# A graph attention and slice attention layer: the first attention's product in seven parts, its residual added by a transfer, and passes moved to ScalarE

## The chip, the core and the metric

The kernel runs on one core of a Trainium2 chip. The core has TensorE (matrix products, written to the eight banks of PSUM), VectorE (DVE in the profile), ScalarE (ACT), GpSimd (POOL), SyncE (SP), which here issues nearly all transfers, and 16 DMA engines that carry them. Each engine works through its own queue of instructions in order; semaphores hold an instruction back until what it needs is there. The metric is the device time of one execution in microseconds (us), as the median of a few runs. A profile is one further execution, recorded by the hardware.

## What is computed

The input x is 32 batches of 512 rows with 256 features, in 32-bit floats. Each batch goes through a graph part (two attentions over 512 nodes, the second masked with a 512 x 512 adjacency) and a slice attention with 8 heads of 64 slices. Both parts have a layer norm before them and x added behind.

```python
def _gat(inp, adj_mask, W, a):
    h = jnp.matmul(inp, W)
    F_ = h.shape[-1]
    f1 = jnp.matmul(h, a[:F_, 0])
    f2 = jnp.matmul(h, a[F_:, 0])
    e = jax.nn.leaky_relu(f1[:, :, None] + f2[:, None, :], ALPHA)
    if adj_mask is not None:
        e = jnp.where(adj_mask[None, :, :] > 0, e, NEG_INF)
    att = jax.nn.softmax(e, axis=2)
    h_prime = jnp.einsum('bij,bjf->bif', att, h)
    return jax.nn.elu(h_prime)
...
out = jax.nn.relu(jnp.matmul(x, mlp1_w) + mlp1_b)            # 256 -> 512
residual = out
out = _gat(jax.nn.relu(out), None, W_fc, a_fc)               # 512 x 512 nodes, 512 features
out = jax.nn.elu(out) + residual
out = jax.nn.relu(jnp.matmul(out, mlp2_w) + mlp2_b)          # 512 -> 256
residual = out
out = _gat(jax.nn.relu(out), adj, W_hand, a_hand)
out = jax.nn.elu(out) + residual
return jax.nn.relu(out)
...
slice_weights = jax.nn.softmax((x_mid @ W_slice + b_slice) / temp, axis=-1)
```

## The kernel before

**Recording and order.** The program first records every operation of all 32 batches (class `Recorder`, from line 52). Its `_cost` gives each operation an estimated duration and its `order` gives each a due time: a step of a batch is due at `TURNS[step]` after the batch's turn, with corrections for the first and last three batches (`HEAD`, `TAIL`). `_schedule` then fills each engine's queue, taking the operation with the smallest due time of those that can start; up to four batches are under way at once. `emit` issues the result. That is why nearly every instruction of the profile has line 290, where the recorded call is made, and why instructions are told apart by their tiles. The order is fixed when the program is built; on the chip each engine keeps it.

**Steps of a batch.** `front` has "load", "norm1", "mlp1", "h", "factors", "p", "pv" and "o1"; `middle` has "mlp2", "h2", "e", "p2" and "pv2"; `back` has "norm2", "w", "sums", "s1T", "tokens", "att", "vo", "gg" and "out". A matrix of 512 x 512 lies in SBUF as four blocks of 128 rows. A matmul takes a 128 x 128 block of weights and up to 512 moving columns; in 32-bit floats the profile shows two records for it.

**The first attention.** "mlp1" (line 686) makes o0T, features by nodes, which is also the residual; o0T has two buffers. "h" multiplies it with W_fc by one level of Strassen's scheme: a 2 x 2 split of both matrices, four mixed left blocks in `mix`, three mixed right blocks made once, and seven products in place of eight, whose results are copied (ScalarE) or added (VectorE, `total`) into the four parts of h. h carries one column more per half, 257 in place of 256: the products with `a` (f1, f2), and later ones, whose product is the softmax's sum. "factors" and "p" make the unnormalised softmax, transposed, as pT. "pv" is the product of pT and h: four blocks of rows, two halves of columns, four matmuls each, 32 in all, into eight PSUM tiles. Behind each block of rows, `elu_elu` scales by the reciprocal sum (one half on VectorE, one on ScalarE), takes the minimum with zero (VectorE), two exponentials (ScalarE) and the maximum (VectorE).

**Transposing by transfer.** In batches 1 to 30 `by_dma` holds: `flip` transposes blocks of 32 x 32 on VectorE into `u_stage`, and `gather` sends that in four pieces to a scratch tensor in DRAM and fetches it back in one transfer, by which blocks find their places. All five are issued by SP. In step "o1" VectorE then adds o0T to the fetched o1T, four sums of 512 columns. In batches 0 and 31 TensorE transposes and VectorE adds from PSUM. The same way goes for xn, e, o2, w and xn2.

**The second layer.** "mlp2" is a Strassen product too: four mixes of o1T, 14 matmuls of 256 columns, copies and totals into o2T, then four Relu with bias.

**The softmax of the slices.** In "w" VectorE takes the maximum of each head from PSUM, subtracts it (512 columns from PSUM to w), ScalarE takes the exponential of 512 columns, and VectorE sums, inverts and multiplies.

**Buffers the change touches.** Tiles with the same tag share buffers and follow each other. mix and pT share one buffer, e has four, o0T two, o1T one.

Of the kernel before, what the change touches and what calls it, by code (L numbers as in the profile page):

```python
# [10 lines left out]
AF = mybir.ActivationFunctionType  # L11
# [6 lines left out]
    "load": 1919.6, "norm1": 757.9, "mlp1": 2922.4, "h": 2999, "factors": 2963.5, "p": 3012.6,  # L18
    "pv": 3019, "o1": 3053.1, "mlp2": 3049.1, "h2": 3076.9, "e": 3079.2, "p2": 2878.8,
    "pv2": 3103.9, "norm2": 3107.9, "w": 3170.3, "sums": 3226, "s1T": 3182.8, "tokens": 3948.3,  # L20
    "att": 792.6, "vo": 1634.2, "gg": 326.4, "out": 996.7,
}
PERIOD, SPARE = 90.53, 0.01

HEAD = (
    (0, 381, 5, 16, 257, -146, -491, -92, -529, -621, 0, 137, -13, -48, 1, 767, 207, -242, -12,
     -51, -10, 0),
    (48, -35, -193, -5, -10, -46, 13, -151, 0, 3, 22, 0, -244, -13, -5, -639, 0, -3, -392, 11,
     -308, -28),
    (-12, 15, 17, -10, 254, 207, -865, 717, -1593, -13, -52, 114, 999, -101, -3, 681, 388, 0,  # L30
     -5, 0, -8, 0),
)
TAIL = (
    (-89, -112, -430, -582, 0, 0, -4, -68, 3, 0, -3, 0, -177, -19, 464, -878, 0, -636, -1, -19,
     33, 129),
    (-70, -57, -31, 0, 0, 0, -514, 1, 23, 200, 0, 0, -677, -169, 954, 2258, 106, -118, 57, -5,
     558, -59),
    (-4, 0, 55, 279, 38, 67, -544, -56, -8, 104, -113, 0, -104, 1, 0, 1, -53, -242, -3, 20, 48,
     166),
# [7 lines left out]
P = 128  # L47
# [4 lines left out]
class Recorder:  # L52
# [5 lines left out]
    ISSUE, BEGIN, LAND, BEHIND = 0.45, 2.2, 0.0, 3.6  # L58
# [69 lines left out]
    def _cost(self, op, out, ins):  # L128
# [6 lines left out]
        if op.method == "dma_start":  # L135
            side = next(ap for ap in (out, *ins) if ap.space != bass.MemoryType.DRAM)
            kb = out.size() / 256
            if side.ap[0][1] <= P // 4:
                op.moving = 0.3 + max(0.0, 1.08 * (kb / 128 - 1))
            else:  # L140
                op.moving = max(1.5 * kb / 512, 4.0 * kb / 1024 - 0.5)
            return self.ISSUE, 0.0
# [7 lines left out]
        if op.engine == "scalar":  # L150
            pointers = sum(isinstance(op.kwargs.get(k), bass.AP) for k in ("bias", "scale"))
            return 0.06 + n / 1200 + 0.09 * pointers + 0.19 * ("accum_out" in op.kwargs), 0.12
# [175 lines left out]
def adj_ffn_kernel(  # L328
# [71 lines left out]
    def gather(what, stage, dst):  # L400
# [5 lines left out]
        for a in range(P // Q):  # L406
# [3 lines left out]
        nc.sync.dma_start(  # L410
            dst, scr.rearrange("(k c) r a j -> (c r) k (a j)", c=P // Q)
        )
# [82 lines left out]
    mixed2 = new("mixed2", [P, 3, 2, P])  # L495
# [691 lines left out]
```

## Time and profile before

| what | value |
|---|---|
| median of 3 runs | 2523.22 us (2522.84 to 2527.05) |
| the profiled execution | 2525.8 us |
| its span, first to last instruction | 2524.0 us |
| mean granted TensorE clock | 0.994 |
| instructions | 35133 |
| DMA | 348.75 MB, 138 GB/s on average, queue 1 busy 49.2% |

The profile names an instruction by engine, operation and tiles, "output<-inputs"; groups add all instructions with the same names. A line of the timeline has the start, the duration, the engine, the line of the program, the operation and how many instructions are merged. In the rows of a group stand the time busy in all, the mean of one in ns, and the idle time before them with what ended it. In the table by stage each row gives the stage's length and, for each engine, its busy time and its instructions, then the granted TensorE clock, the DMA share and GB/s. PEld is the loading of weights, which overlaps PE. SPq is SP's queue, which issues transfers.

### The profile page before, as it was taken

The numbers are of one execution on the slowest core, as the hardware profiler recorded it, in microseconds if no ns is written. First come the engines' busy times: TensorE is split into PE (matmuls) and PEld (weight loads), VectorE is DVE, ScalarE is ACT, GpSimd is POOL, SyncE is SP. The second block draws the span as 40 slices with busy tenths as digits, with TensorE's granted clock in tenths as the row PEclk, the third lists the DMA queues.
The fourth block names the chain that finished last, engine by engine and source line by source line (L and its number), as shares of the span: only waits on it lengthen the run. The fifth ranks groups of instructions, "written<-read, shape, count | busy, mean of one in ns | idle before, by whom it ended". The sixth has DMA issues, their size and how long they took to land.

```text
span 2524.0 us, 35133 instructions
## 1 busy us (share of the span) xinstructions
PE 2470.2 (98%) x12037; PEld 1797.5 (71%) x12037; DVE 2193.6 (87%) x5593; ACT 1175.2 (47%) x2197; POOL 96.3 (4%) x167
## 2 busy tenths in 40 slices
PE   6999999999999999999999999999999999999998
PEld 4867677776777777777777776767777777767674
DVE  7779898998989988889998989988899888989784
ACT  2544444444445444445444444444454454454452
POOL 0000000000000000000000000000000000000000
PEclk8999999999999999999999999999999999999998
DMA  5133555454655445565454654546554455554431
GB/s 173 40 92 101 146 169 158 136 142 113 170 161 165 121 129 143 159 171 142 127 152 130 169 159 136 141 113 171 161 166 120 135 140 157 169 158 123 125 89 53
DMA packets 451144, 348.75 MB, mean 138 GB/s; under 512 B 110228, under 2 KB 375572, under 8 KB 450966
## 3 DMA queue, kind: packets, MB, share of 16 engines
q1 hardware_dynamic: 449382, 345.46, 49.2%
q8 instruction: 96, 1.57, 0.3%
q10 hardware_dynamic: 1584, 1.05, 0.1%
q14 instruction: 82, 0.67, 0.1%
HBM read 186.92 MB, written 159.45 MB: 137 GB/s over the span
## 4 chain that ended last, share of the span: by engine, by line
PE 77%; DMA 9%; DVE 8%; ACT 3%; SPq 1%; issue 1%; POOL 0%; DVEq 0%; ACTq 0%
PE mm L290 74%; PE tr L290 3%; DMA line<-norm 2%; DMA xn_raw<-scr 2%; DMA scr<-u_stage 1%; SPq L290 1%; DVE mix L290 1%; DVE u L290 1%; ACT m L290 1%; DVE xn_stage L290 1%; DVE xn L290 1%; DMA p2T<-scr 1%; DVE m L290 1%; DMA scr<-xn_stage 0%; DMA w<-in_L_gnn_mlp_w_dram 0%
## 5 line engine op out<-in xcount | busy, mean ns | idle before, releaser
L290 PE MATMUL mm<-h,pT 128*128 128x257 f32 (+1 forms) x2048 | 478.5, 379 | 1.3 <-DVE pT L290 1.3
L290 PEld LDWEIGHTS mm<-h,pT 128*128 128x128 f32 x2048 | 384.8, 189 | 106.5 <-issue 44.1
L290 PE MATMUL mm<-weff,xn2T 128*128 128x512 f32 x512 | 254.0, 603 | 0.5 <-ACT xn2T L290 0.5
L290 PE MATMUL mm<-w,xn 128*128 128x512 f32 x512 | 251.5, 595 | 0.5 <-DVE w L290 0.5
L290 PE MATMUL mm<-h,p2T 128*128 128x257 f32 x1024 | 242.6, 380 | 1.0 <-DMA p2T<-scr 1.0
L290 PE MATMUL mm<-xnT,w 128*128 128x512 f32 x512 | 236.3, 604 | 3.0 <-DMA xnT<-scr 2.3
L290 PE MATMUL mm<-gg,wT 128*128 128x256 f32 x1024 | 232.9, 383 | 1.6 <-DVE gg L290 1.6
L290 PEld LDWEIGHTS mm<-gg,wT 128*128 128x128 f32 x1024 | 192.3, 191 | 45.8 <-DVE gg L290 18.8
L290 PEld LDWEIGHTS mm<-h,p2T 128*128 128x128 f32 x1024 | 193.7, 190 | 42.8 <-issue 14.7
L290 ACT ACTIVATE m<-m 128x512 f32<-128x512 f32 x192 | 121.1, 631 | 188.6 <-DVE m L290 188.5
L290 PEld LDWEIGHTS mm<-xnT,w 128*128 128x128 f32 x512 | 94.7, 192 | 114.3 <-issue 99.6
L290 DVE TENSOR_TENSOR h<-mm,h 128x257 f32<-128x257 f32 x320 | 127.2, 417 | 45.9 <-PE mm L290 39.7
L290 DVE SCALAR_TENSOR_TENSOR u<-m,u 128x512 f32<-128x512 f32 x192 | 131.4, 684 | 38.9 <-ACT m L290 38.4
L290 ACT ACTIVATE u<-mm,rd 128x256 f32<-128x256 f32 x192 | 90.3, 470 | 154.8 <-PE mm L290 97.3
L290 ACT COPY h<-mm 128x257 f32<-128x257 f32 (+1 forms) x256 | 95.1, 374 | 130.4 <-PE mm L290 126.2
L290 ACT ACTIVATE w<-w 128x512 f32<-128x512 f32 x128 | 80.1, 626 | 142.4 <-DVE w L290 139.5
L290 ACT ACTIVATE m<-m,neg 128x512 f32<-128x512 f32 x192 | 138.5, 722 | 4.8
L290 ACT ACTIVATE o0T<-mm,b 128x512 f32<-128x512 f32 x128 | 87.7, 685 | 106.3 <-PE mm L290 105.6
L290 PEld LDWEIGHTS mm<-w,xn 128*128 128x128 f32 x512 | 94.9, 189 | 57.1 <-issue 44.0
L290 PE MATMUL mm<-wfc,mix 128*128 128x257 f32 x512 | 133.1, 380 | 0.0
L290 ACT COPY xn2T<-xn_raw 128x512 f32<-128x512 f32 x60 | 34.2, 616 | 202.3 <-DMA xn_raw<-scr 202.3
L290 PE MATMUL mm<-mixed,mix 128*128 128x257 f32 x512 | 125.0, 384 | 0.1
(172 smaller groups left out, 4515.7 us busy)
## 6 DMA issues: line engine op xcount, KB each, us to landing
scr<-xn_stage SPq DMA_DIRECT2D x240, 128.0 KB, 2.7
scr<-u_stage SPq DMA_DIRECT2D x120, 256.0 KB, 4.9
o1T<-scr SPq DMA_DIRECT2D x30, 1024.0 KB, 7.4
scr<-e_stage SPq DMA_DIRECT2D x120, 256.0 KB, 4.7
p2T<-scr SPq DMA_DIRECT2D x30, 1024.0 KB, 6.6
scr<-w_stage SPq DMA_DIRECT2D x120, 256.0 KB, 3.9
w_raw<-scr SPq DMA_DIRECT2D x30, 1024.0 KB, 7.9
x<-in_x_dram SPq DMA_DIRECT2D x32, 512.0 KB, 5.2
```

What stands on the lines that cost most here:

```text
L290: getattr(getattr(self.nc, op.engine), op.method)(*op.args, **op.kwargs)
```

## The change

- "pv" becomes a Strassen product as well: four mixes of pT in a new tile pmix, seven products (28 matmuls), copies on ScalarE and totals on VectorE into four tiles v, which share their buffers with e. pmix takes the buffer of o0T in batches 1 to 30, and o0T has one buffer in place of two. "h" builds the four right blocks that this needs directly (the tile hx), by another order of sums, and the column of ones becomes ones, minus ones and ones in three blocks.
- The residual: in batches 1 to 30 "mlp1" has ScalarE write its result a second time, with columns rearranged, into o1T, which now has two buffers; the gather of u goes out on GpSimd's queue with an add, and the four sums of "o1" are gone.
- "mlp2" loses its Strassen level: 8 matmuls of 512 columns, with o1T's columns read in another order, and two Relu. The mixes of its weights in the setup are gone.
- `elu_elu`: in both attentions the minimum goes from VectorE to ScalarE (a Relu of the negative, then an Exp with scale -1); the first attention's scaling is one pass on ScalarE.
- The softmax of w: no subtraction; for each head ScalarE takes an exponential of 64 columns from PSUM with the negative maximum as bias, 8 for each block of rows. One of "factors"' two products of 512 columns goes to ScalarE.
- Some small tiles share other buffers; `TURNS`, `HEAD`, `TAIL` and the estimates of `_cost` have other values, so the order of every queue differs.

```diff
-    def gather(what, stage, dst):
+    def gather(what, stage, dst, op=None):
...
-        nc.sync.dma_start(
-            dst, scr.rearrange("(k c) r a j -> (c r) k (a j)", c=P // Q)
-        )
+        whole = scr.rearrange("(k c) r a j -> (c r) k (a j)", c=P // Q)
+        if op is None:
+            nc.sync.dma_start(dst, whole)
+        else:
+            nc.gpsimd.dma_start(dst, whole, accum_op=op)
...
-    def elu_elu(parts, m, u):
-        (v0, rd0, cols0), (v1, rd1, cols1) = parts
-        nc.vector.tensor_scalar(u[:, cols0], v0, rd0, None, op0=OP.mult)
-        nc.scalar.activation(u[:, cols1], v1, AF.Copy, scale=rd1)
-        nc.vector.tensor_scalar(m, u, 0.0, None, op0=OP.min)
-        nc.scalar.activation(m, m, AF.Exp)
+    def elu_elu(m, u, to=None):
+        nc.scalar.activation(m, u, AF.Relu, scale=-1.0)
+        nc.scalar.activation(m, m, AF.Exp, scale=-1.0)
         nc.scalar.activation(m, m, AF.Exp, bias=neg1)
-        nc.vector.scalar_tensor_tensor(u, m, -1.0, u, op0=OP.add, op1=OP.max)
+        nc.vector.scalar_tensor_tensor(
+            u if to is None else m, m, -1.0, u, op0=OP.add, op1=OP.max
+        )
...
-        o0T = new("o0T", [P, KH, N], bufs=2)
+        o0T, o1T = new("o0T", [P, KH, N]), new("o1T", [P, KH, N], bufs=2)
...
             nc.scalar.activation(o0T[:, m, :], pm, AF.Relu, bias=b1[:, m : m + 1])
+            if by_dma("u", b):
+                nc.scalar.activation(
+                    swapped(o1T[:, m, :]), pm.rearrange("p (t a i) -> p t a i", t=NT, i=Q),
+                    AF.Relu, bias=b1[:, m : m + 1],
+                )
...
+        keep(h1, product(l11, r11))
+        total(h11, product(l12, r21), h1)
+        keep(h2, product(s3, t3))
+        total(h1, product(s2, t2), h1)
+        total(h1, h1, h2)
+        total(h22, product(s1, t1), h1)
+        total(h3, h2, product(s4, r22), OP.subtract)
+        total(h21, product(l22, t4), h1)
+        total(h2, h11, h3)
+        total(h1, h22, h2, OP.subtract)
+        total(h4, h21, h2, OP.subtract)
...
+        l11, l12, l21, l22 = (pT[:, ts(k, 2), ts(t, 2 * P)] for t in range(2) for k in range(2))
+        held = by_dma("u", b)
+        pmix = new(
+            "pmix", [P, 4, 2, 2 * P], tag="o0T" if held else "o1T", bufs=1 if held else 2
+        )
...
+        keep(v12, product(l11, h11))
+        total(v11, product(l12, h21), v12)
+        keep(v22, product(s1, h1[:, :, :HH]))
+        total(v12, product(s2, h2), v12)
+        for i in range(2):
+            nc.vector.tensor_copy(v21[i][:, HH:], v12[i][:, HH:])
+        total(v21, product(s3, h3[:, :, :HH]), v12)
+        total(v12, narrow(v22), v12)
+        total(v22, narrow(v21), v22)
+        total(v12, product(s4, h22[:, :, :HH]), v12)
+        total(v21, product(l22, h4[:, :, :HH]), v21)
         for i in range(NT):
-            pms = [mm_tile([P, HH + 1]), mm_tile([P, HH])]
-            for s, pm in enumerate(pms):
-                for j in range(NT):
-                    nc.tensor.matmul(
-                        pm, pT[:, j, ts(i)], h[:, j, s, : HH + 1 - s],
-                        start=(j == 0), stop=(j == NT - 1),
-                    )
             rd = small("rd", [P, 1])
...
-            gather("u", stage, o1T)
-            for m in range(KH):
-                o1 = o1T[:, m, :].rearrange("p (t a i) -> p t a i", t=NT, i=Q)
-                nc.vector.tensor_tensor(o1, o1, swapped(o0T[:, m, :]), op=OP.add)
+            gather("u", stage, o1T, OP.add)
...
+        for m in range(KD):
+            pm = mm_tile([P, N])
+            for k in range(KH):
+                nc.tensor.matmul(
+                    pm.rearrange("p (a t i) -> p a t i", t=NT, i=Q), w2[:, k, ts(m)],
+                    swapped(o1T[:, k, :]), start=(k == 0), stop=(k == KH - 1),
+                )
+            nc.scalar.activation(o2T[:, m, :], pm, AF.Relu, bias=b2[:, m : m + 1])
...
-            nc.vector.tensor_reduce(mx, pm3, axis=AX.X, op=OP.max)
-            nc.vector.tensor_tensor(
-                w3, pm3, mx[:, :, None].to_broadcast([P, HEADS, G]), op=OP.subtract
-            )
-            nc.scalar.activation(wt, wt, AF.Exp)
+            nc.vector.tensor_reduce(mx, pm3, axis=AX.X, op=OP.max, negate=True)
+            for hd in range(HEADS):
+                nc.scalar.activation(w3[:, hd], pm3[:, hd], AF.Exp, bias=mx[:, hd : hd + 1])
```

## The prediction

> **What bounds the kernel now.** I read the page's totals first, then busy time by stage, then the order of matmuls in one steady stretch, then the waits, then the transfers around the step that changes.
>
> ```profile
> PE 2470.2 (98%) x12037; PEld 1797.5 (71%) x12037; DVE 2193.6 (87%) x5593; ACT 1175.2 (47%) x2197; POOL 96.3 (4%) x167
> ...
> 0.00:300.00 300.00, 273.35 (x1219) 204.15 (x1220) 240.23 (x626) 126.97 (x238) 11.76 (x26) 0.97 0.41 113
> ...
> 1000.00:1700.00 700.00, 695.10 (x3378) 504.83 (x3377) 623.13 (x1584) 334.76 (x623) 26.69 (x45) 1.00 0.52 144
> ...
> 2200.00:2524.00 324.00, 306.98 (x1598) 218.65 (x1596) 255.79 (x641) 140.03 (x266) 8.99 (x16) 0.98 0.39 109
> ```
>
> TensorE is busy 98% of the span. In the middle stage it idles 4.9 us of 700; nearly all of its idle time is at the start (26.7 us of the first 300) and the end (17.0 of the last 324). The clock granted in the middle is 1.00. So time is the number of matmul columns, plus the two ends. A busy PE isn't yet a PE at its peak, so I price matmuls by the distance between starts:
>
> ```profile
> 1225.76 1.88 PE L290 MATMUL mm<-weff,xn2T 128*128 128x512 f32 x4
> 1227.48 0.38 PE L290 MATMUL tr<-ident,sc 128*128 128x128 f32 x2
> ...
> 1257.99 7.11 PE L290 MATMUL mm<-h,p2T 128*128 128x257 f32 x32
> 1264.94 1.88 PE L290 MATMUL mm<-w,xn 128*128 128x512 f32 x4
> ...
> 1283.41 1.89 PE L290 MATMUL mm<-o1T,w 128*128 128x256 f32 x8
> 1285.14 1.89 PE L290 MATMUL mm<-mix,mixed 128*128 128x256 f32 x8
> ```
>
> One matmul of the program is two records. 512 columns: (1227.48 - 1225.76) / 2 = 0.860 us. 257 columns: 6.95 / 16 = 0.434. 256 columns: 1.73 / 4 = 0.432. Time follows columns; only a change in columns, or a new wait, moves the end.
>
> ```profile
> PE mm L290 <- DVE o1T L290: 2.5, 4, 1.0
> ...
> 1263.36 4.75 SPq L290 DMA_DIRECT2D scr<-u_stage  x4
> ...
> 1271.42 0.37 SPq L290 DMA_DIRECT2D o1T<-scr  x1
> ...
> scr<-u_stage SPq DMA_DIRECT2D x120, 256.0 KB, 4.9
> o1T<-scr SPq DMA_DIRECT2D x30, 1024.0 KB, 7.4
> ```
>
> The transposed blocks of the first attention go out in four pieces and come back in one transfer. They are in time today: the second layer's matmuls waited 2.5 us in the whole run for o1T. But between the last product (timeline: 1257.99) and mlp2 (1283.41) lie only 25.4 us of other matmuls, and o1T's sums run at 1279.92: this is the tight place.
>
> **The change, part by part.**
>
> *TensorE.* The product of the first attention goes from 32 matmuls per batch to 28: 4 x 0.434 = 1.74 us less. mlp2 loses its own Strassen level: 14 matmuls of 256 (14 x 0.432 = 6.05 us) become 8 of 512 (8 x 0.860 = 6.88), 0.83 us more. Over 32 batches: -55.6 + 26.6 = -29.0 us. mlp2's moving operand is now read in blocks of 32 columns, which no row shows; between no effect and the 2% by which 257 columns vary here I take none (upper end +0.14 us a batch, 4 us).
>
> *VectorE.* These rows go or grow:
>
> ```profile
> L290 DVE TENSOR_SCALAR m<-u 128x512 f32<-128x512 f32 x192 | 78.9, 411 | 26.0 <-ACT u L290 25.5
> L290 DVE TENSOR_TENSOR w<-mm,mx 128x512 f32<-128x512 f32 x128 | 87.0, 680 | 0.4
> L290 DVE TENSOR_TENSOR o1T<-o1T,o0T 128x512 f32<-128x512 f32 x120 | 74.9, 684 | 1.8 <-DMA o1T<-scr 1.8
> L290 DVE TENSOR_TENSOR h<-h 128x257 f32<-128x257 f32 x128 | 51.7, 418 | 1.6
> L290 ACT ACTIVATE m<-m 128x512 f32<-128x512 f32 x192 | 121.1, 631 | 188.6 <-DVE m L290 188.5
> L290 ACT ACTIVATE ex<-ex 128x8 f32<-128x8 f32 x32 | 6.5, 202 | 22.0 <-DVE ex L290 22.0
> L290 ACT COPY mean<-mm 128x128 f32<-128x128 f32 x32 | 8.5, 265 | 19.4 <-PE mm L290 19.4
> ```
>
> Gone: o1T's sums 75, mlp2's mixes 85 (128 x 0.66) and totals 94, the minimum m<-u 79, two thirds of u<-mm,rd 60, the subtraction of w 87, acb 22: 502 us. Added: pmix 128 x 0.66 = 85, totals of v 448 x 0.40 = 179, h's totals from 448 to 576, 128 x 0.40 = 51, small ones 18: 333. Net -169: 2194 becomes some 2025, 80%. It was not the bound and moves further away. I cost this at nothing: TensorE's rows cover it. Were that cover gone, VectorE would set 2025 us, still less.
>
> *ScalarE.* Added: Relu for the minimum 192 x 0.631 = 121; the second copy of mlp1 (the residual) 120 x 0.685 = 82; acb 19; four copies of v a batch 48; the scaling of v 22 net; mlp2's two wide instead of six narrow ones -41. The softmax of w goes from 128 wide exponentials (80) to 1024 of 64 columns; no row is that narrow with a bias. Bounds: 0.20 us (the 8-column row) and 0.36 (the 128-column row plus the 0.09 by which m<-m,neg exceeds m<-m). I take 0.30: +227 (125 to 289). Sum +478: 1175 becomes 1653, 65%. Again under TensorE.
>
> A rule speaks against moving min and max: the Trainium skill, "ScalarE: Activation LUTs", Rules for kernel authors, gives relu, max and min to VectorE. By the rows it is right about price, 0.411 against 0.631; with VectorE at 87% and ScalarE at 47% the dearer engine is the freer one, so the sum by the rule (42 us lost) doesn't reach the end.
>
> *The residual's transfer.* The gather of 1 MB moves from SP's queue to GpSimd's and adds into o1T, where ScalarE has written the residual. On SP it frees one issue of 0.37. Behind it on GpSimd stand the two small operations of each layer norm (1.1 and 0.34 us), which now also wait until the four pieces have landed; the next norm's statistics come later than that in VectorE's order, so nothing. How long an adding transfer takes no row shows. Lower bound: the plain one, 7.4. Upper: two streams read instead of one, 14.8. It is one transfer of the same size between the same places, so I take it nearer the plain end, 8.
>
> The Trainium skill, "DMA: Bandwidth & Descriptors", SWDGE vs HWDGE vs iDMA, says only GpSimd's queue can accumulate; its fit for that queue (2.0 us plus bytes at 436 GB/s) would give an estimate of 4.4 us, under the plain row. "SBUF — State Buffer", SBUF: two separate sides, warns that VectorE's two-port operations hold up that queue's descriptors; by it the transfer would be later, and no row here shows it.
>
> Is it in time? After the last product the built order has 19 matmuls of 512 and 26 of 257 before mlp2: 16.3 + 11.3 = 27.6 us, some 28.4 at the middle's real pace (two batches lie 152.6 us apart in the chain of waits, 615.62 to 768.26, where these prices give 148.4). Against it: tiles 0 and 1 are ready about 0.8 us before the end of the last product (1.74 of matmuls still to come, less two totals and a reciprocal); ScalarE then runs four passes for four tiles (scale, Relu, two Exp: 0.64 + 0.63 + 0.63 + 0.72 = 2.63 each), 10.5, with some 2 us of w's narrow ones in between; VectorE's max and transposition of the last 1.4: 13.1 after the last product. Four issues of 0.46 and 4.9 to land: 6.7. The transfer, 8. Together 27.8. It just fits; I cost it at nothing, and name the price below.
>
> *The ends.* In batches 0 and 31 the transpositions of u are TensorE's and no longer interleave with the product's rows: all four tiles come after it. ScalarE's 10.5 us then stand against 7.8 us of other matmuls in batch 0 (8 x 0.86 and 8 transpositions) and about 2 in batch 31, where before only the last row's 3.6 stood open: +3 and +5 us. The setup loses five small VectorE operations (2.0 us), hidden by the loads. Together +8 (0 to +16).
>
> *Sum.* -29 + 8 = -21. The profiled execution took 2525.8 us, its span 2524.0 and 1.8 around it; it becomes 2504.8. The median of the runs is 2523.2, 2.6 under it: **2502**.
>
> **Rivals.** *The adding transfer is late* (the slower side). Place: mlp2's first matmul, in order on TensorE with everything behind it; nothing takes up a wait there, since the middle stage has 0.7% idle. Price: 30 batches x each us past 28.4, so beyond 8.6 us for the transfer the wait begins, and at 9.3 the 21 us are gone. Midway between its bounds, at 11, it is 2.4 late: 72 us, 2574. At 14.8, 6.2 late: 186, 2688. For it: the slack is under 1 us, and three 1 MB gathers share the queues there. Against: today's chain is as tight and waits 2.5 us in all.
>
> *The gain is eaten inside the product.* Seven products need 14 PSUM tiles per batch, each drained by a copy (0.37) or total (0.40) before the next sums; before, 8 with looser order. If each batch waits 0.7 us more, the time is 2523. Against: VectorE is 7 points freer, and the same scheme for h costs PE waits of only 0.2 us in the whole run.
>
> *More than the columns.* VectorE's relief also closes waits at the ends: no loss there and a quarter of their 43.7 idle us gone, 2523 - 29 - 11 = 2483.
>
> *The product isn't shorter at all*: ruled out by the built order, 28 matmuls where 32 stood.
>
> **How the numbers follow.** My forecast 0.54, more than the columns 0.10, eaten inside 0.14, late transfer 0.22. Anything within 0.2% (5 us, about what a measurement of this kernel can tell from no change) is the middle of the third case. Faster: 0.54 + 0.10 + 0.03 = 0.67; same 0.07; slower 0.22 + 0.04 = 0.26. Range: from 2480 to 2580, which takes in the late transfer up to some 2.5 us a batch; the likeliest case alone is 2490 to 2514.
>
> **What would show it.** Right: PE's records of the product 1792 instead of 2048 and mlp2's 512 of 512 columns, spacing unchanged; the middle's batches some 75.4 us apart; DVE near 80%, ACT near 65%; the page's issue list giving o1T<-scr under 8.6 us; no PE wait on o1T. Wrong: a PE wait on DMA o1T<-scr of over 1 us a batch, or PE under 97% in the middle stage.

## The result, and the profile after

The changed kernel takes 2695.35 us, median of 4 runs (2683.12 to 2701.47), against 2525.14 for the kernel before beside it (2522.84 to 2527.7): a ratio of 1.0671, with a 95% interval of 1.0637 to 1.0704. The forecast was 2502, the range 2480 to 2580. The profiled execution took 2690.28 us, its span 2688.5; with the forecast of 2504.8 for such an execution, 185.5 us are to be found.

The totals of the page, and the table by stage (length, then busy time and instructions of PE, PEld, DVE, ACT and POOL, the granted clock, the DMA share, GB/s), of the changed kernel:

```profile
PE 2496.1 (93%) x11397; PEld 1700.3 (63%) x11397; DVE 2029.3 (75%) x5532; ACT 1482.0 (55%) x3437; POOL 129.3 (5%) x197
...
0.00:300.00 300.00, 272.69 (x1177) 192.74 (x1178) 230.08 (x645) 161.81 (x343) 15.68 (x29) 0.98 0.45 115
1000.00:1700.00 700.00, 653.57 (x2929) 442.53 (x2928) 526.58 (x1436) 386.49 (x898) 35.41 (x52) 0.97 0.55 137
2364.50:2688.50 324.00, 295.67 (x1483) 199.17 (x1481) 226.19 (x593) 172.30 (x426) 10.70 (x18) 0.96 0.42 106
```

In the middle 700 us TensorE idles 46.4 us where it idled 4.9, and its clock is 0.97 where it was 1.00. By share of the whole span no engine has become the bound: TensorE and VectorE are less busy than before, and ScalarE is at 55% (by stretches of a batch it is another matter, as the experiments show). The loss is waits, and a batch takes 82.7 us (mlp1's starts, batch 4 to 28) where it took 76.5.

The waits of TensorE in the changed kernel (us in total, times, longest), then one of VectorE, then three transfers (count, KB each, median us from issue to landing):

```profile
PE mm L297 <- DMA o1T<-scr: 99.1, 26, 6.1
PE mm L297 <- DVE w L297: 27.6, 23, 2.4
PE mm L297 <- ACT xn2T L297: 11.0, 7, 6.7
...
DVE norm L297 <- DMA norm<-s1T: 168.1, 27, 8.8
...
scr<-u_stage SPq DMA_DIRECT2D x120, 256.0 KB, 4.5
o1T<-scr POOLq DMA_DIRECT2D x30, 1024.0 KB, 12.1
norm<-s1T SPq DMA_DIRECT2D x32, 2.0 KB, 10.4
```

The last of these transfers in the kernel before:

```profile
norm<-s1T SPq DMA_DIRECT2D x32, 2.0 KB, 4.5
```

(w is the softmax of the slices, xn2T the transposed result of the second layer norm.) The adding transfer takes 12.1 us where the plain one took 7.4, and mlp2 waits for it 99.1 us in all. A transfer of only 2 KB that SP issues beside it lands after 10.4 us; before it took 4.5. One batch of the changed kernel shows both. First the timeline (start, duration), then the table by stage for the stretches around the wait:

```profile
1315.89 1.89 PE L297 MATMUL mm<-hx,pT 128*128 128x256 f32 x8
...
1333.12 0.70 DVE L297 STREAM_TRANSPOSE u_stage<-m 128x512 f32<-128x512 f32 x1
1333.85 3.36 SPq L297 DMA_DIRECT2D scr<-u_stage  x4
...
1341.53 1.36 POOL L297 DMA_DIRECT2D o1T<-scr  x1 [21.92 <-ACT o1T L297]
...
1343.54 1.82 SPq L297 DMA_DIRECT2D norm<-s1T  x1
...
1353.59 3.75 PE L297 MATMUL mm<-o1T,w 128*128 128x512 f32 x4 [3.85 <-DMA o1T<-scr]
1354.00 0.17 DVE L297 TENSOR_SCALAR norm<-norm 128x4 f32<-128x4 f32 x1 [6.57 <-DMA norm<-s1T]
```

```profile
1341.50:1349.70 8.20, 8.20 (x31) 5.36 (x29) 1.80 (x4) 5.93 (x12) 1.49 (x2) 1.00 0.99 167
1349.70:1353.60 3.90, 0.05 (x2) 0.04 (x1) 0.00 (x0) 0.37 (x1) 0.00 (x0) 0.89 0.82 162
1353.60:1357.10 3.50, 3.50 (x4) 1.47 (x5) 3.10 (x9) 0.00 (x0) 0.00 (x0) 0.50 0.49 153
```

The last product ends at 1317.8, the last transposition at 1333.8 (16.0 us later, 3 more than in the median batch), the adding transfer is issued at 1341.5 and lands 11.9 later. For the last 3.9 us hardly an engine has work: TensorE stands at mlp2, VectorE at norm, in order, and both are released within half a microsecond. Then TensorE runs at half clock: this stretch lasts 6.83 us from 1352.7 on, and TensorE is at work in 5.9 us of it. This happens in nearly every batch: the trace has 31 stretches at half clock, 156.8 us in all, against 5 and 31.8 before. Of the 31, 18 are 3.41 us long and 9 are 6.83. The Trainium skill, "TensorE: Matmul & The Clock Gate", Part 1: The HAM clock gate, says that a free-running window of some 3.4 us without work halves the clock. The lengths agree with such a window. That it has to be without work does not show here, and the measurement decides: in the 3.41 us before each of the 31 drops TensorE was at work for 0 to 1.53 us, 0.74 in the median.

The difference of the spans, 2688.5 - 2524.0 = 164.5 us, is made up so: fewer columns, -29.0; TensorE's idle time (span less busy) from 53.8 to 192.4, +138.6; half clock, +51.7, since TensorE is at work in 125.5 us of the stretches at half clock, against 22.2 before, and does half as much in them: (125.5 - 22.2) / 2. In the rest of these stretches it stands anyway. The sum is 161.3, 3 short.

### The profile page after: what moved, and what is told of

Read it like the earlier page. It is cut to its first block, busy times and chain, and to the rows that moved or that the text cites. A ratio compares the mean times of both kernels' runs of the same rounds, so it can differ in the third digit from the quotient of the medians.

```text
span 2688.5 us, 35257 instructions
## 1 busy us (share of the span) xinstructions
PE 2496.1 (93%) x11397; PEld 1700.3 (63%) x11397; DVE 2029.3 (75%) x5532; ACT 1482.0 (55%) x3437; POOL 129.3 (5%) x197
## 3 DMA queue, kind: packets, MB, share of 16 engines
q0 software_dynamic: 15840, 31.46, 6.7%
## 4 chain that ended last, share of the span: by engine, by line
PE 50%; DVE 24%; DMA 18%; issue 3%; ACT 3%; SPq 1%; POOL 0%; DVEq 0%; POOLq 0%; ACTq 0%
PE mm L297 48%; DMA o1T<-scr 9%; DVE e L297 4%; DVE pT L297 2%; DMA norm<-s1T 2%; DVE v L297 2%; PE tr L297 2%; DVE e_stage L297 2%; DVE xn_stage L297 1%; DVE pmix L297 1%; DVE xn L297 1%; DMA xn_raw<-scr 1%; DMA scr<-e_stage 1%; DVE mx L297 1%; SPq L297 1%
## 5 line engine op out<-in xcount | busy, mean ns | idle before, releaser
L297 PE MATMUL mm<-o1T,w 128*128 128x512 f32 x512 | 273.9, 694 | 101.5 <-DMA o1T<-scr 99.1
L297 PE MATMUL mm<-w,xn 128*128 128x512 f32 x512 | 245.8, 604 | 28.3 <-DVE w L297 27.6
L297 ACT ACTIVATE w<-mm,mx 128x64 f32<-128x64 f32 x1024 | 249.7, 341 | 33.8 <-DVE mx L297 30.3
L297 PEld LDWEIGHTS mm<-o1T,w 128*128 128x128 f32 x512 | 111.4, 224 | 247.2 <-issue 243.1
L297 PE MATMUL mm<-h,p2T 128*128 128x257 f32 x1024 | 235.1, 383 | 2.1 <-DMA p2T<-scr 1.2
L297 ACT ACTIVATE v<-v,rd 128x512 f32<-128x512 f32 x128 | 85.7, 712 | 211.9 <-DVE rd L297 211.9
L297 ACT COPY wT<-w_raw 128x512 f32<-128x512 f32 x120 | 65.4, 615 | 239.2 <-DMA w_raw<-scr 239.2
L297 PEld LDWEIGHTS mm<-weff,xn2T 128*128 128x128 f32 x512 | 88.3, 191 | 69.7 <-issue 48.7
L297 PE MATMUL mm<-h,pT 128*128 128x257 f32 x512 | 126.3, 390 | 4.0 <-DVE pT L297 4.0
L297 PE MATMUL mm<-wfc,mix 128*128 128x257 f32 x512 | 126.5, 379 | 1.5 <-DVE wfc L297 1.5
L297 DVE TENSOR_TENSOR v<-mm,v 128x256 f32<-128x256 f32 (+1 forms) x320 | 124.2, 413 | 4.5 <-PE mm L297 4.3
## 6 DMA issues: line engine op xcount, KB each, us to landing
o1T<-scr POOLq DMA_DIRECT2D x30, 1024.0 KB, 12.1
```

Source lines behind the costliest of these rows:

```text
L297: getattr(getattr(self.nc, op.engine), op.method)(*op.args, **op.kwargs)
```

## The experiments

The runs with no interval given are single executions; the kernel before took 2522.5 to 2528.9 us beside them. They are set against the profiled execution of the changed kernel, 2690.3; its four runs lie 18 us apart, so that less than that tells nothing. "Left out" means that the output isn't the reference's. The edits are shown shortened to the operations that are issued in place of others; where the text says "in the same order", every queue keeps the changed kernel's order.

### What the fetch costs

The fetch of o1T without the add: e1 on the same queue, e2 on SP's as before. Both leave the residual out of the second layer's input in batches 1 to 30.

```diff
-            nc.gpsimd.dma_start(dst, whole, accum_op=op)
+            nc.gpsimd.dma_start(dst, whole)     # e1
+            nc.sync.dma_start(dst, whole)       # e2, at the same place of the order
```

> The fetch of u goes out on GpSimd's queue as in the changed kernel and in the same place, but without the add; the residual of the first attention is so left out. Every queue has the same order. In the changed kernel the fetch takes 12.1 us, TensorE waits 99.1 us for it in all, and its clock stands at half for 157 us (32 before), which costs about half of the 125 more, 62 us. Theory A (the add makes the transfer long): it lands in 7 to 9 us, TensorE waits under 15 us on o1T, the mean clock is 0.99 again, and the span is 2688 - 99 - 62 = 2527, give or take 20. Theory B (the queue is slow, not the add): 11 us or more, and the span stays within 1% of 2688. Theory C (the rest of the chain, four tiles on ScalarE after the whole product, is what is late): the wait moves to another tile and the span stays over 2600.

> As the run before, without the add (the residual is left out), but SP issues the fetch, at the place in its queue that the order of issue gives; all other queues as in the changed kernel. Theory A: like the run on GpSimd's queue, 7 to 8 us to landing, span 2527 give or take 20. Theory B: 7.4 us here and 2527, with 12 on GpSimd's queue. Theory C: over 2600. If SP's later pieces of w are held up behind it, waits on w grow and the span is some 20 us above the run on GpSimd's queue.

Measured: e1 2616.8 us, e2 2558.8. The waits of TensorE and the transfer, of e1 and of e2:

```profile
PE mm L297 <- ACT xn2T L297: 39.9, 26, 3.9
PE mm L297 <- DVE w L297: 28.0, 23, 2.6
PE mm L297 <- DMA o1T<-scr: 24.4, 22, 1.7
...
o1T<-scr POOLq DMA_DIRECT2D x30, 1024.0 KB, 9.3
```

```profile
PE mm L298 <- ACT xn2T L298: 28.6, 25, 3.7
PE mm L298 <- DVE w L298: 25.5, 23, 2.1
...
o1T<-scr SPq DMA_DIRECT2D x30, 1024.0 KB, 6.5
norm<-s1T SPq DMA_DIRECT2D x32, 2.0 KB, 5.7
```

No theory holds for both runs: the transfers land near theory A's 7 to 9 and 7 to 8 us, but neither time is within 20 us of its 2527; e1's is over 2600 as in theory C, with xn2T as the longest wait, e2's fits none. The add is worth 2.8 us a transfer and 73 us of time, GpSimd's queue in place of SP's another 2.8 and 58 us. With the short transfer the wait for o1T is gone, but the kernel is still 55 us above its forecast of 2504.8, and TensorE waits for xn2T and w.

What the 12.1 us are made of: half of the fetch on GpSimd's queue, half on SP's, with the add on GpSimd's half (e11) and without (e14). Half of the residual, or all of it, is left out.

```diff
+                self.nc.gpsimd.dma_start(dst[:, :2], whole[:, :2], **op.kwargs)   # e14: without the add
+                self.nc.sync.dma_start(dst[:, 2:], whole[:, 2:])
```

> The changed kernel with half of the fetch adding (the first 512 KB, on GpSimd's queue) and the other half plain on SP's queue; half of the residual isn't added to the second layer's input in batches 1 to 30. It asks what the 12.1 us are made of. By bytes alone (12.1 x 1/2) the adding half would land in 6 to 7 us; by a fixed part, as the nearest rows have it (9.3 us for the plain 1 MB on this queue, 6.5 on SP's), in 9 to 10; if contention with other transfers sets it, in 11 or more. The time follows from the landing: about 2570 to 2600 us at 7, 2620 to 2640 at 9.5, 2670 or more at 11.

> The run with half of the fetch on GpSimd's queue and half on SP's, now both plain (none of the residual is added in batches 1 to 30). With the run before it, it divides the price of the add: 512 KB took 8.1 us adding and 1 MB 12.1, so 4.0 us for 512 KB and 4.1 fixed; 1 MB plain took 9.3 on GpSimd's queue and 6.5 on SP's. If adding doubles the price by bytes and the queue adds a fixed part, 512 KB plain on GpSimd's queue lands in 6.5 to 7.5 us (some 4.5 to 5.5 fixed and 2 to 2.4 by bytes); if the queue itself is slow by bytes, in 5 to 6.

Measured: e11 2604.1 us, e14 2557.6. The transfers of e11, then of e14:

```profile
o1T<-scr SPq DMA_DIRECT2D x30, 512.0 KB, 4.6
o1T<-scr POOLq DMA_DIRECT2D x30, 512.0 KB, 8.1
```

```profile
o1T<-scr SPq DMA_DIRECT2D x30, 512.0 KB, 4.9
o1T<-scr POOLq DMA_DIRECT2D x30, 512.0 KB, 6.5
```

| fetch | 512 KB | 1 MB | per 512 KB | the rest |
|---|---|---|---|---|
| SP, plain | 4.6 to 4.9 | 6.5 | 1.6 to 1.9 | 2.7 to 3.3 |
| GpSimd, plain | 6.5 | 9.3 | 2.8 | 3.7 |
| GpSimd, adding | 8.1 | 12.1 | 4.0 | 4.1 |

(The halves ran beside the other half, so the split is an estimate.) The add goes mostly by bytes: 4.0 us for 512 KB against 2.8 on the same queue, and more than twice SP's. The time follows the landing: e11, at 8.1, lies between what was expected at 7 and at 9.5.

The add at another place, nothing left out: ScalarE's queue fills the scratch tensor with the residual, and the four pieces of u go out adding; the fetch is plain on SP's queue (the core of the edit):

```diff
+                self.nc.scalar.dma_start(self.whole[b], o1T)
-            nc.sync.dma_start(scr[:, :, a, :], stage[ts(a, Q)])
+            nc.gpsimd.dma_start(scr[:, :, a, :], stage[ts(a, Q)], accum_op=op)
-            nc.gpsimd.dma_start(dst, whole, accum_op=op)
+            nc.sync.dma_start(dst, whole)
```

> The changed kernel with the add at another place of the same way, nothing left out: ScalarE's queue sends the residual from o1T to the scratch tensor beforehand (1 MB), the four pieces of 256 KB go out on GpSimd's queue with the add, and the fetch is plain on SP's queue. Theory A (an adding transfer pays by its bytes, and only the last piece lies on the path): the fetch lands in 6 to 7 us, the last piece lands 2 to 3 us later than its 4.5, mlp2's wait for o1T under 25 us, 2560 to 2610. Theory B (an adding transfer on this queue pays by its issue and by sixteen queues kept busy, whatever its size): the four pieces together cost as much as the one, the time stays at 2680 or more.

Measured: 2775.0 us. The fetch landed after 6.0 us and the pieces after 6.4, about as theory A had it, and o1T held TensorE only 31.7 us, but the time is far above A's; now xn2T held it 119.6, and SP, where the fetch waits in order for the pieces, stood 177.0 us for them. The wait has moved. That SP's standing is what makes xn2T late was not tried; this way also moves 31 MB more in all.

### Can the wait be stepped over?

The first run, e3_late15, raised the planner's estimate of the adding transfer (line 139, issue and length), so that it would place mlp2 later by itself; the second, e3_mlp2_later, moved mlp2's matmuls by hand behind the next batch's h product and kept all else. Nothing is left out in either.

```diff
-                return (0.1, 3.1) if op.engine == "scalar" else (1.0, 5.0 + 3 * kb / 1024)
+                return (0.1, 3.1) if op.engine == "scalar" else (1.3, 12.0 + 3 * kb / 1024)   # e3_late15
```

> The changed kernel with one number of the order's estimates raised: the adding transfer is taken to need 15 us in place of 8, so the whole order is planned anew and mlp2 stands some 47 us of other matmuls behind the last product, a batch further on. Theory A: no wait on o1T, clock at 0.99, span 2500 to 2560, depending on what the new order costs elsewhere. Theory C: over 2640. If this order is under 2524, the change was worth its columns and only its order was planned on a wrong duration.

Measured: 4590.8 us, with the period of a batch at 148 us and waits everywhere. I take it that `TURNS` and the other due times fit one set of estimates, and that the order falls apart when one of them is changed; that was not tried further. The estimate of 1.0 + 8.0 us by which the changed kernel's own order was planned is some 3 us short of the 12.1. The run shows one thing more of the transfer:

```profile
o1T<-scr POOLq DMA_DIRECT2D x30, 1024.0 KB, 9.8
```

With 76 GB/s of traffic on average, where the changed kernel has 130, the same adding transfer lands after 9.8 us. So the 12.1 isn't the price of the transfer alone; how much of it the traffic beside it costs in the changed kernel was not separated.

> The changed kernel with its adding transfer, nothing left out, but in batches 6 to 27 the 8 matmuls of mlp2 stand behind the next batch's h product on TensorE: 18 more matmuls of 257 columns, 7.8 us more cover. The transfer arrives 32.6 us after the last product (13.0 to the last transposition, 7.5 to the issue, 12.1 to landing), the cover becomes 27.6 + 7.8 = 35.4. Theory A (it is the arrival against the cover): no wait on o1T in these 22 batches, and their share of the 161 us comes back, 118: 2570, give or take 20. Theory C (another part of the chain or another engine takes its place): over 2640, with the wait under another name. The next layer's Relu now stands bare before h2, some 1 us a batch at most.

Measured: 2722.1 us, as theory C had it. A line of its waits:

```profile
PE mm L309 <- DVE mix L309: 115.1, 24, 6.8
```

mlp2 no longer waited (9.2 us), but the next batch's mixes did: VectorE makes them behind its two operations on norm, and it still waited 171.7 us for the 2 KB transfer. So that wait was moved as well: VectorE's two operations on norm behind the next batch's transpositions of norm2, alone (e5), with mlp2 (e6), and with both and the plain fetch on SP (e7, the residual left out).

```diff
+        for engine, step, ahead, behind, ages in (("tensor", "mlp2", 1, "h", (6, 28)), ("vector", "s1T", 1, "norm2", (4, 28))):
+            for age in range(*ages):
+                late = [op for op in done if op.engine == engine and (op.age, op.step) == (age, step)]
+                wait = [op for op in done if op.engine == engine and (op.age, op.step) == (age + ahead, behind)]
...
+                done[at:at] = late
```

> The changed kernel with one thing moved and nothing left out: in batches 4 to 27 VectorE's two small operations on norm (which wait for the 2 KB transfer norm<-s1T beside the adding transfer, 5.3 us a batch in the changed kernel's profile) stand behind the next batch's flips of norm2 instead of ahead of them. Theory A (mlp2's wait for the adding transfer is what each batch pays for; VectorE's wait lies beside it): the time stays at 2688 us, 2675 to 2705, PE still waits for DMA o1T<-scr 85 to 105 us, and VectorE's wait on norm falls from 168 to under 60 us. Theory B (VectorE's in-order wait makes the chain behind it late, and that chain feeds the next product): 2600 to 2660, and the wait on o1T falls too.

> Both moves together, nothing left out: mlp2's matmuls behind the next batch's h product (batches 6 to 27) and VectorE's two operations on norm behind the next batch's flips of norm2 (batches 4 to 27). Theory A (the adding transfer costs in two places, on TensorE at mlp2 and on VectorE at norm, and each hides the other): with both places moved the period falls from 82.5 to some 77 us, the time to 2540 to 2590, and neither o1T nor mix holds TensorE over 20 us in all. Theory B (the changed kernel has no room for 12 us anywhere in its order; a third place takes the wait over): over 2640 us, and the table of waits names the new one.

> Both moves together, and the fetch plain on SP's queue, so the residual isn't added to the second layer's input in batches 1 to 30. It shows what the order costs without the add. If the adding transfer is all that stands between the changed kernel and the predicted 29 us of columns: 2500 to 2525 us, PE waits under 50 us in all. If the waits on xn2T (28.6 us) and w (25.5 us) of the run with the plain fetch alone are the change's other cost (the narrow exponentials of w, and passes moved to ScalarE): 2535 to 2570, with these two waits still there at 20 us or more each.

Measured: e5 2702.4, e6 2690.6, e7 2613.0 us. e5's time and VectorE's wait on norm (15.1 us) are as its theory A had them; o1T still holds TensorE 75.2 us, less than A's 85, and waits for xn (24.0) came in its place. Of e6's theories B was right; its waits:

```profile
PE mm L327 <- ACT xn2T L327: 69.1, 24, 4.9
PE mm L327 <- DVE w L327: 26.1, 23, 2.2
PE mm L327 <- ACT hx L327: 24.7, 22, 2.9
```

o1T holds TensorE 9.8 us and the time is the same. The moves have a price of their own, 54 us with the short transfer (e7 against e2), which neither expectation of e7 had; with the add they give about as much as they cost.

### What the rest is

With the fetch as short as before 55 us were open. First theory: the eight narrow exponentials of w. e8 (on e2, residual left out) and e9 (on the changed kernel, nothing left out) went back to the subtraction and one wide exponential, in the same order:

```diff
-            nc.vector.tensor_reduce(mx, pm3, axis=AX.X, op=OP.max, negate=True)
-            for hd in range(HEADS):
-                nc.scalar.activation(w3[:, hd], pm3[:, hd], AF.Exp, bias=mx[:, hd : hd + 1])
+            nc.vector.tensor_reduce(mx, pm3, axis=AX.X, op=OP.max)
+            nc.vector.tensor_tensor(w3, pm3, mx[:, :, None].to_broadcast(list(w3.shape)), op=OP.subtract)
+            nc.scalar.activation(wt, wt, AF.Exp)
```

> The run with the plain fetch on SP's queue (2558.8 us; the residual isn't added to the second layer's input in batches 1 to 30) with one more part of the change undone, in the same order of every queue: the softmax of w subtracts the maximum on VectorE and takes one exponential of 512 columns, in place of eight of 64 from PSUM. Theory A (the eight narrow exponentials are what is left: TensorE waited 25.5 us for w and 28.6 us for xn2T there): both waits fall under 8 us each, the half clock with them, 2505 to 2530 us. Theory B (they only hold w, whose wait is too short to cost clock): the wait for w falls, the one for xn2T stays, 2530 to 2550. Theory C (the waits come from the order, not from the exponentials): 2550 to 2570 us.

> The changed kernel with that softmax of w undone alone, nothing left out, the add as in the changed kernel. If the add's wait and the exponentials' wait add up: some 25 to 30 us off, 2655 to 2670. If the wait for the adding transfer takes up what w gives: 2680 to 2700 us, and PE's wait for DMA o1T<-scr grows from 99 to about 125 us.

Measured: 2653.6 and 2776.7 us, 95 and 86 more, where no theory expected more than 2570 and 2700. The 84 us of VectorE's time that came back (2029.3 to 2113.3 with the add) appear in full in the time, though VectorE is at 76%; TensorE's wait for w grew to about 48 us, and one of 29.7 us for another tile of VectorE's, top, came. So it was no clean test of the exponentials. e15 (on e2) and e16 (on the changed kernel) take their number away and add nothing: one maximum for the whole row, one exponential of 512 columns from PSUM; the softmax is the same.

```diff
+            nc.vector.tensor_reduce(mx[:, :1], pm, axis=AX.X, op=OP.max, negate=True)
+            nc.scalar.activation(wt, pm, AF.Exp, bias=mx[:, :1])
```

> The run with the plain fetch on SP's queue (2558.8 us; the residual isn't added to the second layer's input in batches 1 to 30), with the eight narrow exponentials of w replaced by one of 512 columns from PSUM, in the same place of every queue and with nothing added on VectorE: the softmax takes the maximum of the whole row in place of each head's (the result is the same, since a shift cancels). There TensorE waited 25.5 us for w. Theory A (the narrow exponentials, some 2.0 us for each block of rows, make w late, and undoing them the old way failed because of the subtraction that came back on VectorE): the wait for w falls under 8 us, and the time by 25 to 45 us, to 2515 to 2535. Theory B (w is late because VectorE's sums and products are): the wait stays within 20 to 30 us, 2550 to 2560.

> The changed kernel with the same exponential of the whole row alone, nothing left out, the add as it is. If the waits for w and for the adding transfer add up: 25 to 40 us off, 2650 to 2665. If mlp2's wait for o1T takes up what w gives: 2675 to 2700, with that wait at 115 us or more.

Measured: 2579.7 and 2705.3 us, both above what was expected: 21 us more, and 15 more, which is within the spread. TensorE's wait for w stayed at 27.3 and 26.6 us, as theory B had it. The number of exponentials isn't what makes w late. The 21 us are the difference of two single runs, and I have no cause for them.

Then VectorE's in-order wait for the 2 KB transfer, taken away by letting its two operations work on a constant tile, in the same order: on e2 (e12) and on the changed kernel (e13). The slices' norm is left out of the result.

```diff
-        nc.vector.tensor_scalar(norm, norm, 1e-5, None, op0=OP.add)
-        nc.vector.reciprocal(norm, norm)
+        nc.vector.tensor_scalar(still, still, 1e-5, None, op0=OP.add)
+        nc.vector.reciprocal(still, still)
```

> The run with the plain fetch on SP's queue (2558.8 us; the residual isn't added to the second layer's input in batches 1 to 30), with VectorE's wait for the 2 KB transfer norm<-s1T taken away and every queue's order kept: in batches 1 to 30 VectorE's two small operations on norm work on a constant tile, so that the slices' norm isn't added to and inverted. There VectorE waited 65.7 us for it in the whole run, and TensorE 28.6 for xn2T and 25.5 for w. Theory A (VectorE stands in order behind that transfer, and this is what makes w and xn2T late): both PE waits fall under 10 us, the half clock from 42 to some 32 us, 2500 to 2515 us, which is where the columns put it. Theory B (w and xn2T are late for another reason): the waits stay, 2545 to 2560.

> The changed kernel with the same wait taken away and the add as it is (in batches 1 to 30 the slices' norm isn't added to and inverted). VectorE waited 168 us for norm<-s1T there, and TensorE 99 for o1T. If the adding transfer alone pays at mlp2: 2675 to 2700 us with PE waiting 95 to 125 us for o1T. If VectorE's wait, which the add lengthens from 4.5 to 10.4 us of landing, makes the chain in front of the transfer late too: 2620 to 2660.

Measured: e12 2545.3, e13 2680.4 us. The waits of e12, then of e13:

```profile
PE mm L300 <- DVE w L300: 29.2, 24, 2.6
PE mm L300 <- ACT xn2T L300: 13.4, 15, 3.7
```

```profile
PE mm L299 <- DMA o1T<-scr: 68.7, 18, 5.4
PE mm L299 <- DVE xn L299: 31.4, 8, 4.4
```

In e12 the wait for xn2T halved and the one for w stayed; neither theory was right. VectorE's wait explains xn2T in part, not w. (The 13.5 us by which the time fell are less than the 18 that tell nothing; the waits are the evidence.) With the add there, VectorE's 168 us are nearly free. e13's time is as the first expectation had it, its wait for o1T is not: that fell from 99.1 to 68.7 us, and a wait of 31.4 us for xn, a tile of VectorE's, came in its place.

What makes w late stands in e2's trace. The table by stage for one period of a batch, cut where TensorE gets w:

```profile
1234.40:1264.60 30.20, 29.17 (x146) 21.10 (x144) 30.11 (x86) 19.49 (x47) 1.35 (x2) 1.00 0.49 131
1264.60:1311.80 47.20, 46.17 (x207) 30.68 (x208) 33.16 (x90) 26.43 (x62) 1.37 (x3) 1.00 0.60 158
```

In the 30.2 us before, VectorE (the third busy time) is at work for 30.11, in the order of its queue, and the last of this work is the product that makes this block of w; TensorE stands 1.07 us for it. In the other 47.2 us VectorE has 14 us to spare. At 18 of e2's 23 waits for w VectorE had worked for 30 us or more with no break over 0.15 us, at four more for 10. So for this part of each batch VectorE is the bound, though it is at 79% over the run. No run takes work out of this stretch, so what that is worth in time is not shown; that e8's added work costs in full fits it.

### The add alone undone

e18 computes everything: the fetch is plain on SP, in four pieces into the buffers of v and e, and VectorE adds the residual to o1T in four sums, ahead of mlp2. e17 is the same with the row's maximum.

```diff
-            nc.gpsimd.dma_start(dst, whole, accum_op=op)
+            raw = [new("raw_u", [P, N], tag="e", bufs=4) for k in range(KH)]
+            for k in range(4):
+                nc.sync.dma_start(raw[k], whole[:, k])
+            for k in range(4):
+                nc.vector.tensor_tensor(dst[:, k], dst[:, k], raw[k], op=OP.add)
```

> Nothing left out: the run with the row's maximum and the plain fetch on SP's queue, with the residual added again by VectorE. The fetch goes out in four pieces of 256 KB into the buffers of v and e, idle then, and four sums of 512 columns (0.68 us each) add them to o1T, standing about 3.5 us ahead of mlp2 in VectorE's order. If the sums fit into the 2.5 us between the landing and mlp2, as the run with the plain fetch has them: within 10 us of e15, 2520 to 2545, and the whole change is worth its columns but for the add. If they hold mlp2 or VectorE: 2560 to 2620, with PE waiting for DVE o1T some 30 to 60 us.

> Nothing left out: the changed kernel with the residual's add alone undone. The fetch is plain on SP's queue, in four pieces of 256 KB into the buffers of v and e, and VectorE adds them to o1T in four sums of 512 columns, some 3.5 us ahead of mlp2 in its order; the softmax of w is the changed kernel's. The run with the row's maximum was 20.9 us slower than the one without, so this one should take that much less than the 2624.4 of the same sums with it: 2595 to 2610 us, PE's waits for xn2T, o1T and w at 25 to 45 us each, and none for a transfer of o1T. If the add by transfer were all that is wrong with the change, it would be 2500 to 2525, below the kernel before; if the sums take away what the plain fetch gives, 2640 or more.

Measured: e17 2624.4 us; e18 2622.9, median of 4 runs (2618.1 to 2624.4), a ratio to the kernel before of 1.0385 (1.0367 to 1.0402). The profiled execution of e18:

```profile
PE 2460.3 (94%) x11397; PEld 1685.7 (64%) x11397; DVE 2099.5 (80%) x5652; ACT 1481.9 (57%) x3437; POOL 89.2 (3%) x167
...
PE mm L313 <- ACT xn2T L313: 45.7, 25, 3.3
PE mm L313 <- DVE w L313: 26.0, 23, 2.1
PE mm L313 <- DVE o1T L307: 22.9, 23, 2.3
```

Undoing the add gives back 72 of the 170 us (medians, 2695.4 and 2622.9). e17 lies just above its second case, e18 between its forecast and its last case: VectorE's sums, 69 us of work, and the fetch in four pieces, which was not tried without them, cost 64 against the plain fetch alone (2558.8), and the row's maximum makes no difference here. As in e8, work added to VectorE in this order shows in the time. No version tried beats the kernel before.

## Why the prediction was wrong, step by step

**The columns: right.** The product has 1792 records where it had 2048, mlp2 has 512 records of 512 columns. The median distance of two records is 429 ns for mlp2 with its strided operand and 429 for mlp1's product; 256 and 257 columns stand at 215 to 217, as before. The strided reading costs nothing.

**The adding transfer: the step that failed.** I wrote "It is one transfer of the same size between the same places, so I take it nearer the plain end, 8." It took 12.1, in the upper half of my bounds. The rest of that chain held within 1 us (medians over 30 batches):

| step | forecast | measured |
|---|---|---|
| last product to last transposition | 13.1 | 13.0 |
| to the issue | 6.7 | 7.6 |
| the transfer | 8 | 12.1 |
| sum | 27.8 | 32.7 |
| cover until mlp2 | 28.4 | 29.1 |

So mlp2 stands 3.6 to 3.9 us in nearly every batch (26 times). The way to the issue alone took 0.9 us more than forecast, which is more than the slack of 0.6, and the cover was 0.7 longer: with 8 us for the transfer mlp2 would just have been in time, because these two happen to cancel. The reason that I gave for the upper end, two streams in place of one, was the nearer one for the part by bytes (4.0 us for 512 KB against SP's 1.6 to 1.9), and I did not price the queue apart from the add, though it was 58 of the 131 us. The estimate of 4.4 us by the fit of "DMA: Bandwidth & Descriptors", Anatomy of one DMA, in the Trainium skill stands against 9.3 plain and 12.1 adding on that queue: the measurement decides. The same page, Rules for kernel authors, says that an accumulating transfer reads its destination and writes it later. More time by bytes fits that; on the same queue it was 1.4 times as much (4.0 against 2.8), not twice. Nor did VectorE's operations make the transfer long, which I named as a possible hold-up of that queue: VectorE is at work for 1.8 us of its 12.1 in the changed kernel, and for 6.4 of its 12.0 in e13 (medians).

**The price of being late: right at mlp2, too low in all.** At 12.1 my rival's rule gives (13.1 + 6.7 + 12.1 - 28.4) x 30 = 105 us, 2607; mlp2's wait measured 99.1. That 2688, the rival's time at 14.8 us, is near the measured one is luck. Place and mechanism were right; what the rule left out is the half clock behind such waits (some 52 us in all) and TensorE's other idle time, 39.5 us more than before, with 27.6 for w and 11.0 for xn2T in it. e1 shows the same: o1T holds TensorE 24.4 us there, near the 21 of the rule at 9.3 us, but the time is 112 us above the forecast.

**"Behind it on GpSimd ... so nothing": the wrong queue.** The norm operations on GpSimd did no harm: VectorE waited 41.0 us for their result, 42.3 before. What the adding transfer delayed stood on SP's queue: norm<-s1T, from 4.5 to 10.4 us, with VectorE in order behind it. It is hidden while o1T is later (e13), and takes over as soon as mlp2 is moved (e3_mlp2_later).

**VectorE and ScalarE "at nothing": the sizes, not the reading.** VectorE: 2025 forecast, 2029.3 measured. ScalarE: 1653 forecast, 1482.0 measured; the narrow exponentials took 250 in place of 307, within my bounds. The rest is overlap: the rows of ScalarE's tiles add up to 1643.5 us, 1223.5 before, and records of neighbours overlap more than before, which the busy time counts once. But a free 20% of VectorE is no slack: some 85 us added to it cost 95 and 86 us (e8, e9), and 54 us of e2 are left with hardly a wait for o1T. "TensorE's rows cover it" was read from the average and from the old order, in which TensorE waited for VectorE almost nowhere in the middle; in the new one VectorE works some 30 us of each batch without a break, and TensorE waits for w behind it even with a short fetch. This is the second step that failed, the smaller one.

**The ends: within the bounds, not in the parts.** By mlp1's first matmul, e2 is 11.0 us faster than the kernel before up to batch 4, and 16.1 slower from batch 28 on: +5.1 together. These stretches hold eight batches, whose columns are some 7 us fewer, so the ends cost some +12 where I had +8 (0 to 16). In the changed kernel, whose last batches also wait for the add, it is -10.1 and +26.0.

**What stays open.** From 2690.3, the add on its queue is 73 us, that queue 58, VectorE's wait 13.5 (single runs, and the last less than their spread); this leaves e12 at 2545.3, 40.5 us above the forecast. It has 42.6 us of waits for w and xn2T. w is late, some 1.2 us in each of 24 batches, behind VectorE's unbroken work; neither the number of exponentials nor the 2 KB transfer is it. What holds xn2T for the 13.4 us that are left, and how much time a shorter queue on VectorE would give back, stays open.

## What to carry to other kernels

An edit that puts a new kind of transfer on a tight path should be priced at the far end of its bounds until a run has shown it, queue, operation and the traffic beside it apart: here 1 MB cost 6.5 us on SP's queue, 9.3 on GpSimd's and 12.1 there with an add. In this kernel, where the slack was under a microsecond, waits cost more than their length: the clock fell behind them (99.1 us of waits came with some 52 us lost at half clock), and the in-order queues beside them shifted. The share of an engine over a run hides stretches: VectorE at 79% had 30 us in each batch without a break. An order planned ahead of time is part of the kernel: a move by hand (2722.1 us) or one changed estimate (4590.8 us) can cost more than the wait that it was to remove.

## What the runs showed of the hardware

The adding transfer goes out in nearly twice the packets: 15840 for 31.46 MB, against 8160 for the same bytes without the add. The rows of the transfer queues (packets, MB, share of 16 engines' span), of the changed kernel, then of e1:

```profile
q0 software_dynamic: 15840, 31.46, 6.7%
```

```profile
q0 software_dynamic: 8160, 31.46, 4.0%
```

Issuing it keeps GpSimd for 1.34 us, 0.83 without the add. A transfer of 2 KB from SP's queue that runs beside a 1 MB fetch slows with it: 5.7 us beside SP's plain fetch, 7.9 beside GpSimd's, 10.4 beside the adding one; 4.0 in e18, where the fetch goes in four pieces of 256 KB.
